# RWKV layers: the outer products of mixes and decays as float32r matmuls over stacked halves, and a product kept in PSUM

## The chip, the cores and the metric

One NeuronCore of a Trainium2 chip runs the whole program. The metric is device time in microseconds (us) of one execution; smaller is better. A matmul runs on TensorE (PE), which loads its weights with a separate instruction (PEld) that can run beside a matmul. VectorE is DVE, ScalarE is ACT, GpSimd is POOL, and SyncE (SP) issues the transfers (DMAs). Each engine works through its own list in order and waits on semaphores for the others.

## What is computed

Input `x` has 16 sequences of 100 steps and 512 channels; `ctx_2048` has 16 sequences of 361. Four layers follow one another: a cross attention with a layer norm (layer 0), an RWKV block (layer 1), a second cross attention with an FFN (layer 2), another RWKV block (layer 3). The change is in the two RWKV blocks only. Cut to what matters, such a block is:

```python
xa = ln(x);  sx = shift(xa) - xa
xxx = tanh((xa + sx * maa_x) @ maa_w1).reshape(b, l, 5, 32)
xxx = einsum('blfd,fde->blfe', xxx, maa_w2)          # five "outer products", 32 deep
xk, xw, xv, xr, xg = xa + sx * (maa_stack + xxx)
w = exp(-exp(time_decay + tanh(xw @ td_w1) @ td_w2)) # one more, 64 deep
r, k, v = xr @ Wr.T, xk @ Wk.T, xv @ Wv.T;  g = silu(xg @ Wg.T)
# per head of 16 channels, over the 100 steps: a = k v^T; out = r (u a + s); s = a + w s
x1 = x + groupnorm(out) * g @ Wo.T
rr = sigmoid(xr2 @ Wfr.T);  kk = relu(xk2 @ Wfk.T) ** 2   # channel mix on ln(x1)
return x1 + rr * (kk @ Wfv.T)
```

## The kernel before

`rwkv(n, ...)` does one RWKV block; it is called for layers 1 and 3. Sequences go in groups of four (`G = 4`, `NG = 4`), so a group has T = 400 columns, and channels go in four chunks of 128 (`NC = 4`). Activations in the projections stand with channels on the 128 partitions and the 400 steps as columns.

**Units.** The recurrence of one chunk of one group is split into eight units of two value rows each: 4 x 4 x 8 = 128 units to a layer. Unit u does: `spread` (two float32r matmuls of 128 x 128 weights `sel` on 400 columns into PSUM tile `vb`, one unit ahead), `product` (DVE copies the first state into `vb`, L1254, and multiplies `vb` by k in place, L1258), `scan` (two DVE scans into tile `a`, L1267; POOL multiplies `a` by r, L1268), and every second unit `gather` (PE sums `a` over channels into `acc`, L1272). `vb` has two tiles, so `spread(u+1)` waits for the scans of unit u-1. The halves of `v` for `spread` were made in the same manner that the change uses: `plain` (L973) rounds v to float32r (`hi`), DVE makes the rest (`lo`), both go to DRAM, and `enter` (L1206) brings them back stacked on 128 rows.

**Pieces.** All other work on PE is cut into pieces, each with a planned cost in us, a first unit (slot) at which it may be taken, and a function that writes its instructions. The loop over u (L1342) runs from -42; before unit 0 only pieces are written. At each u it writes the unit's instructions, then takes pieces from the head of the list until a budget is used: `due = min(due, 0.0) + (2.9 if 0 <= u < UNITS else 3.9)`, less 0.45 in odd units and 0.7 in units 2 and 7 of a chunk (L1390). Cost 0.0 pieces are taken as soon as their slot comes. All engines' programs follow this order.

`projections(g)` (L872) writes the pieces of one group: layer norm and transposes (`turned`, 0.45 each), `inner` (the `maa_w1` product and its tanh into tile `z0`, L936, 2.7), `mixed` (L943: outer products of a pair of mixes, or of one, then DVE's `tm` and POOL's `xj`), `decay_in` (L995: the `td_w1` product together with the last columns of `maa_w1`; tanh into `tz`, L1020), the projections k, v, r (2.7 each), `decay` (L1026) and, held back for the next group's list, the gates g (`held`, then `behind`, 8 half chains of 1.35). Pieces of `behind` stand before `inner` (four) and between the mixes (0,1).

In `mixed` the weights of mix f lie in rows 32f to 32f+32 of `w2a` (f = 4: rows 96 to 128 of `w2b`) and are multiplied with the same rows of `z0` (`tz`), all in float32. `decay` uses rows 0 to 64 of `w2b` and `tz`. A float32 matmul appears in the trace as two records, a float32r matmul as one.

`channels(g)` (L1087) writes the channel mix of a group: layer norm, `keys`, and row products with `gates_of` and `values` (L1155: DVE multiplies the tanh with the product in PSUM into an SBUF tile, then halves and adds x). It starts (L1361) once all four groups are projected. What is left of the pieces after unit 127 runs in the tail. PSUM has three banks for all pieces (`slots`); a bank is read by DVE or ACT before it is used again. `stage` is a ring of six tiles of 128 x 512 for everything on its way to or from DRAM.

## Time and profile before

| what | us |
|---|---|
| three runs: median (lowest to highest) | 3258.19 (3251.58 to 3261.73) |
| the profiled execution | 3254.77 |
| its span, first to last instruction | 3253.0 |
| PE busy / DVE / ACT / POOL in the span | 2949.2 / 1688.9 / 1192.1 / 1157.3 |
| layer 1 about 664 to 1440, layer 3 about 2488 to 3253 | 776, 765 |
| layer 3: first unit starts, last unit starts | 2607.5, 3171.2 |
| layer 1: first unit starts, last unit starts | 784.2, 1351.9 |

How to read the views: a line of the **windows** view gives a stretch, its length, and for PE, PEld, DVE, ACT and POOL the busy time with the number of instructions, then the share of TensorE's clock that was granted, the DMA share and GB/s. A line of the **timeline** gives start, duration, engine, line, operation, output <- inputs with shapes, and a count where neighbours were merged. A line of the **groups** gives line, engine, operation, shapes, count, then busy time, mean ns of one, and the idle time before it with who ended it. The record of a matmul includes its way through the array, so neighbours overlap and the distance between two starts, not the duration, tells what a matmul costs in a dense stretch. L88 and L93 are lines of helpers, so instructions are told apart by their tiles.

### The profile page before, as it was taken

What the parts mean: (1) busy time and instruction counts of PE and PEld (TensorE: products, weight loads), DVE (VectorE), ACT (ScalarE), POOL (GpSimd) and SP (SyncE); (2) the same over time, 40 slices, a digit from 0 to 9 for tenths busy, and PEclk for the clock granted to TensorE, in tenths of its full rate; (3) what the DMA queues carried; (4) which work ended last, traced back from release to release, by engine and by line L of the source; (5) the groups of instructions that cost most, each with busy time, mean ns of one, the idle gap of its engine ahead of it and who ended that gap; (6) DMA issues with size and microseconds to landing.
All of it is one profiled execution on the core that took longest, in us unless ns stands there. A gap on an engine that the chain in (4) does not pass through costs nothing. (4 is left out here: it accounts for less than half of the span.)

```text
span 3253.0 us, 44092 instructions
## 1 busy us (share of the span) xinstructions
PE 2949.2 (91%) x16403; PEld 1497.6 (46%) x16403; DVE 1688.9 (52%) x3565; ACT 1192.1 (37%) x2627; POOL 1157.3 (36%) x966
## 2 busy tenths in 40 slices
PE   7999899888999988879999999899998899998887
PEld 4555555533444434334555555445554444444443
DVE  2555556634888877533433333321001288887871
ACT  4777677721333333322232223211111223333332
POOL 0111111134768666522212111220001267766662
PEclk9999999987999989879999999999998899998988
DMA  6101010021332522120000010020011322332211
GB/s 196 33 23 33 23 36 23 1 90 51 108 102 78 165 76 82 55 88 20 20 21 20 21 30 23 27 71 7 11 50 31 109 91 71 111 128 84 73 53 52
DMA packets 134690, 193.97 MB, mean 60 GB/s; under 512 B 19807, under 2 KB 102687, under 8 KB 134475
## 3 DMA queue, kind: packets, MB, share of 16 engines
q1 hardware_dynamic: 134474, 191.15, 19.1%
q8 instruction: 129, 2.11, 0.3%
q14 instruction: 87, 0.70, 0.1%
HBM read 115.20 MB, written 49.15 MB: 51 GB/s over the span
## 5 line engine op out<-in xcount | busy, mean ns | idle before, releaser
L88 POOL TENSOR_TENSOR a<-a,rc 128x800 f32<-128x800 f32 x256 | 482.0, 1884 | 290.4 <-DVE a L88 174.1
L88 DVE TENSOR_TENSOR_SCAN a<-wc,vb 128x400 f32<-128x400 f32 x512 | 477.3, 974 | 29.0 <-PE acc L93 2.9
L88 DVE CUSTOM_DVE_ANT_0 pr<-l_sc,mask 100x361 f32<-100x361 f32 x512 | 252.2, 529 | 144.7 <-PE l_sc L93 144.6
L88 ACT ACTIVATE pr<-pr,nm 100x361 f32<-100x361 f32 x512 | 301.2, 593 | 4.6 <-POOL sums L88 3.7
L88 DVE TENSOR_TENSOR vb<-vb,kc 128x792 f32<-128x792 f32 x256 | 253.8, 992 | 8.8
L96 PEld LDWEIGHTS l_pT<-ident,pr 100*121 100x121 f32 x1536 | 193.2, 186 | 103.8 <-issue 50.3
L93 PE MATMUL vb<-xc,sel 128*128 128x400 f32 x512 | 221.0, 515 | 14.8 <-DVE a L88 14.7
L1534 DVE CUSTOM_DVE_ANT_0 junk<-l2a_sc,mask 100x361 f32<-100x361 f32 x256 | 136.9, 535 | 182.6 <-PE l2a_sc L93 164.7
L96 PE MATMUL l_pT<-ident,pr 100*121 100x100 f32 x1536 | 216.3, 276 | 6.2 <-ACT pt L88 4.3
L88 POOL TENSOR_TENSOR xj<-tm,ext 128x400 f32<-128x400 f32 x160 | 151.2, 962 | 106.5 <-DVE tm L88 95.5
L1570 POOL TENSOR_TENSOR pa<-pt,pt 121x1600 f32<-121x1600 f32 x16 | 57.1, 3570 | 363.7 <-ACT pt L1565 363.7
L1755 DVE TENSOR_TENSOR x<-pb,x 100x512 f32<-100x512 f32 x16 | 12.9, 805 | 319.6 <-DMA pb<-po 310.8
L88 ACT COPY pt<-l_pT 121x400 f32<-121x400 f32 x256 | 125.1, 489 | 146.5 <-PE l_pT L96 145.5
L93 PE MATMUL v<-l_v_w,ct 128*121 128x512 f32 x384 | 176.9, 605 | 0.0
L74 PE MATMUL h<-yTb,l_fc 128*128 128x400 f32 x512 | 172.8, 499 | 0.6 <-ACT yTb L339 0.6
L93 PE MATMUL k<-ct,l_k_w 128*128 128x361 f32 x512 | 170.6, 476 | 0.0
L88 DVE SCALAR_TENSOR_TENSOR tm<-mm,vec,sx 128x400 f32<-128x400 f32 x160 | 95.4, 623 | 141.3 <-PE mm L93 135.3
L74 PE MATMUL p<-l_proj,h 128*128 128x512 f32 x384 | 165.5, 592 | 0.0
L93 PEld LDWEIGHTS vb<-xc,sel 128*128 128x128 f32 x512 | 99.6, 204 | 125.8 <-issue 61.7
L88 POOL TENSOR_SCALAR ve<-mv 100x1 f32<-100x1 f32 x16 | 3.6, 223 | 406.8 <-DVE mv L88 406.8
L93 PE MATMUL l_sc<-kz,qz 32*100 32x361 f32 x1024 | 112.2, 508 | 34.3 <-DVE nm L88 32.1
L88 DVE COPY pt<-l_pT 121x400 f32<-121x400 f32 x128 | 73.5, 574 | 130.3 <-PE l_pT L96 68.3
(280 smaller groups left out, 5136.0 us busy)
## 6 DMA issues: line engine op xcount, KB each, us to landing
ct<-in_ctxT SPq DMA_DIRECT2D x32, 722.0 KB
dk<-k SPq DMA_DIRECT2D x32, 200.0 KB
kc<-dk SPq DMA_DIRECT2D x32, 200.0 KB
dv<-v SPq DMA_DIRECT2D x32, 200.0 KB
dhi<-hi SPq DMA_DIRECT2D x32, 200.0 KB
dlo<-lo SPq DMA_DIRECT2D x32, 200.0 KB
dw<-wd SPq DMA_DIRECT2D x32, 200.0 KB
vc<-dv SPq DMA_DIRECT2D x32, 200.0 KB
```

What stands on the lines that cost most here:

```text
L74: nc.tensor.matmul(out=ps, lhsT=lhs(c), rhs=rhs(c), start=(c == 0), stop=(c == n - 1))
L88: return lambda *args, **kw: tc.keep_in_program_order(op(*args, **kw))
L93: pin(nc.tensor.matmul(**kw))
L96: pin(nc.tensor.transpose(out, in_, ident))
L1534: nc.vector.tensor_tensor_reduce(out=junk, in0=ss[r][:L, :S2], in1=t["mask"], scale=-1.0, scalar=FLT_MAX, op0=ALU.add, op1=ALU.min, accum_ ...
L1570: nc.gpsimd.tensor_tensor(t["pa"], t["pt"][0], pt, ALU.add)
L1755: nc.vector.tensor_tensor(x, pb[:, i, :], x, ALU.add)
```

## The change

1. The outer products of the mixes and of the decay become float32r matmuls over 128 rows. Weights and tanh are each split in a float32r number and an exact rest. The rows of a mix are stacked hi, lo, hi, lo against weights hi, hi, lo, lo (32 rows each), which gives all four products in one pass; the decay (64 rows deep) takes two passes, one with the weights' hi, one with their lo.
2. The stacked weights are made in the layer itself: `outer_weights` loads each block of rows broadcast over the partitions (6 DMAs), ACT rounds, POOL subtracts. The loads of `w2a` and `w2b` go.
3. `halves` makes hi (ACT) and lo (DVE) of the tanh, and 16 or 6 DMAs per tanh copy the rows to their places in tile `zs`.
4. The first states `s0` are loaded and centered by group instead of once.
5. `values` multiplies into PSUM, and the second product reads PSUM.
6. The planner: pair of mixes 1.0 to 0.6, single mix 0.9 to 0.3, decay 0.9 to 0.6; the budget of a unit 2.9 to 2.65; all gates of the group before stand between `inner` and the mixes; the layer norm of the channel mix of groups 0 and 1 gets a slot three units earlier, with its products where they were.

```diff
-            vec, w1, w2a, w2b, td1, gwb = (small[k] for k in ("vec", "w1", "w2a", "w2b", "td1", "gwb"))
+            vec, w1, td1, gwb = (small[k] for k in ("vec", "w1", "td1", "gwb"))
+            w2 = one.tile([128, 5, E], F32R, name="w2")
+            td2 = one.tile([128, 2, E], F32R, name="td2")
...
+            def outer_weights(f):
+
+                raw = stage(f"w2_{n}_{f}")
+                if f < 5:
+                    nc.sync.dma_start(
+                        out=raw, in_=d[f"L{n}_maa_w2"][32 * f : 32 * f + 32, :].partition_broadcast(4)
+                    )
+                    hi, lo, rs = w2[:, f, :], w2[64:, f, :], slice(64, 128)
+                else:
+                    nc.sync.dma_start(out=raw, in_=d[f"L{n}_td_w2"].partition_broadcast(2))
+                    hi, lo, rs = td2[:, 0, :], td2[:, 1, :], slice(0, 128)
+                scalar.copy(hi, raw)
+                gpsimd.tensor_tensor(lo, raw[rs], plain32(hi[rs]), ALU.subtract)
...
+                s0 = first_states[g] = two.tile([128, NC, G, 16], F32, tag="s0", bufs=3, name=f"s0_{nm}")
+                nc.sync.dma_start(out=s0, in_=d["s0"][:, :, g * G : (g + 1) * G, :])
...
-                        st["z0"] = two.tile([128, T], F32, tag="z0", bufs=1, name=f"z0_{nm}")
-
-                        st["tz"] = two.tile([128, T], F32, tag="tz", bufs=1, name=f"tz_{nm}")
+                        centered(s0.rearrange("p c b s -> p (c b) s"), 16, f"s{nm}")
...
+                def halves(ps, k):
+
+                    z = two.tile([128, T], F32, tag="tm", bufs=4, name=f"z{k}_{nm}")
+                    st["hi", k], st["lo", k] = (stage(f"z{h}{k}_{nm}")[:, :T] for h in ("h", "l"))
+                    scalar.activation(z, ps[:, :T], AF.Tanh)
+                    scalar.copy(st["hi", k].bitcast(F32R), z)
+
+                    def low():
+                        vector.tensor_tensor(st["lo", k].bitcast(F32R), z, st["hi", k], ALU.subtract)
+                        for fs in ((0, 1), (2, 3)) if k == 0 else ((4, 5),):
+                            t = two.tile([128, 2, T], F32R, tag="zs", name=f"zs_{nm}_{fs[0]}")
+                            for i, f in enumerate(fs):
+                                zs[f] = t[:, i, :]
+                                wide = 64 if f == 5 else 32
+                                r0 = 32 * f if f < 4 else 96 if f == 4 else 0
+                                for q in range(128 // wide):
+                                    nc.sync.dma_start(
+                                        out=plain32(t[wide * q : wide * q + wide, i, :]),
+                                        in_=st[("hi", "lo")[q % 2], k][r0 : r0 + wide],
+                                    )
+
+                    stacked[k] = slots.defer(1, low, True)
...
                 def mixed(fs, c):
 
+                    stacked[fs[0] // 4]()
...
-                        mm(out=ps[:, :T], lhsT=w[rs, cols], rhs=z[rs, :], start=True, stop=True)
+                        mm(out=ps[:, :T], lhsT=w2[:, f, cols], rhs=zs[f], start=True, stop=True)
...
                 def decay(co):
 
+                    stacked[1]()
                     ps = slots.bank()
...
+                    for i in range(2):
+                        mm(
+                            out=ps[:, :T], lhsT=td2[:, i, co * 128 : (co + 1) * 128], rhs=zs[5],
+                            start=(i == 0), stop=(i == 1),
+                        )
...
-                pieces.extend(behind[:4])
+                if not g:
+                    for f in range(6):
+                        piece(0.0, lambda f=f: outer_weights(f), base + 2)
                 inner()
+                pieces.extend(behind)
                 for c in range(NC):
                     mix((0, 1), c)
-                    pieces.extend(behind[4 + 2 * c : 6 + 2 * c])
...
-                slot = base + (3 if pace else 1)
+                slot = base + (1, 3, 6)[pace]
...
-                            vector.scalar_tensor_tensor(th, th, 1.0, got, ALU.add, ALU.mult)
-                            vector.scalar_tensor_tensor(x, th, 0.5, x, ALU.mult, ALU.add)
+                            vector.scalar_tensor_tensor(got, th, 1.0, got, ALU.add, ALU.mult)
+                            vector.scalar_tensor_tensor(x, got, 0.5, x, ALU.mult, ALU.add)
...
-                        channel_stream(g, u + (8, 8, 4, 2)[g], g < NG - 1)
+                        channel_stream(g, u + (5, 5, 4, 2)[g], (2, 2, 1, 0)[g])
...
-                due = min(due, 0.0) + (2.9 if 0 <= u < UNITS else 3.9)
+                due = min(due, 0.0) + (2.65 if 0 <= u < UNITS else 3.9)
```

## The prediction

> **What bounds the kernel now.** I read the page first, then the stretches of one RWKV layer in the windows view (layer 3; layer 1 repeats it to within 3%), then PE's timeline, then the waits. In the windows the columns are PE, PEld, DVE, ACT, POOL busy, the clock granted, the DMA share:
>
> ```profile
> 2490.00:2520.00 30.00, 19.71 (x57) 9.49 (x57) 13.51 (x15) 8.30 (x13) 15.80 (x17) 0.60 0.03 10
> 2520.00:2600.00 80.00, 68.92 (x192) 32.59 (x190) 15.55 (x30) 24.65 (x44) 21.32 (x26) 0.88 0.35 111
> 2607.00:3171.00 564.00, 510.88 (x2124) 235.28 (x2126) 465.61 (x674) 191.62 (x315) 389.27 (x304) 0.93 0.28 88
> 3185.00:3253.00 68.00, 53.82 (x282) 26.84 (x282) 12.14 (x24) 16.70 (x29) 13.08 (x18) 0.92 0.14 43
> ```
>
> The first two rows are what comes before unit 0, the third the 127 steps from unit 0's start to unit 127's, the last the tail. Inside the units PE leads with 511 of 564 us, but DVE has 466. One unit costs 564/127 = 4.44 us; counted from the starts of DVE's copies into `vb`, the shortest are 3.0 to 3.1 us, which is DVE's own chain (0.16 + 0.99 + 1.86). So DVE is idle for 98 us of the 564. Who ends that idle time bounds what a faster PE can give:
>
> ```profile
> DVE vb L88 <- PE vb L93: 38.8, 21, 9.2
> PEld mm L93 <- POOL xk_3b L88: 24.2, 10, 5.7
> DVE tm L88 <- PE mm L93: 7.3, 8, 1.8
> ```
>
> Only 38.8 + 7.3 = 46 us of DVE's idle time end with a PE product. Part of these 46 is not PE's speed: where the channel mix waits for POOL's `xk`, PE stands still and `vb` comes late (the longest wait, 9.2 us, ends at 2986.8, right behind such a stop). I put that part at 20 us.
>
> **What an outer product costs.** The timeline of PE, where one merged row holds several records:
>
> ```profile
> 2522.84 0.94 PE L93 MATMUL mm<-z,maa_w2a 32*128 32x400 f32 x4
> 2523.71 2.95 PE L93 MATMUL mm<-xj,l_Wk 128*128 128x400 f32 x8
> 2526.59 0.94 PE L93 MATMUL mm<-z,maa_w2a 32*128 32x400 f32 x4
> ...
> 2527.47 2.95 PE L93 MATMUL mm<-xj,l_Wk 128*128 128x400 f32 x8
> ...
> 2613.55 1.61 PE L93 MATMUL mm<-xj,l_Wk 128*128 128x400 f32 x4
> 2614.69 0.84 PE L93 MATMUL vb<-xc,sel 128*128 128x400 f32 x2
> 2615.36 1.51 PE L93 MATMUL mm<-xj,l_Wk 128*128 128x400 f32 x4
> ```
>
> Four float32 records last 1.51 us with a last one of 0.50, so they start (1.51-0.50)/3 = 0.336 us apart; a float32 product of 400 columns, two records, costs 0.67. The next `l_Wk` after 2523.71 starts at 2527.47: 3.76 us for eight records (2.69) and one pair of mixes, so **a pair costs 1.06**. The decay (2538.73 to 2542.48) and a single mix (2553.72 to 2557.47) show the same 3.75, so 1.06 each: the two of a pair run beside each other, on different rows. The new form is in the trace already: `vb<-xc,sel` is float32r, 128 x 128 weights, 400 columns. The last `l_Wk` before it starts 0.50 us before 2613.55 + 1.61, at 2614.66, and holds the array until 2615.00; the next starts at 2615.36. Two products cost 0.36, **0.18 each**. The other end is where such a pair stands between small weights: 2617.67 to 2618.23, 0.56 or 0.28 each. The neighbours will mostly be 128 x 128, so I take 0.18.
>
> Per layer there are 32 pairs, 16 single mixes and 16 decays. Saved: 32 x (1.06-0.36) + 16 x (1.06-0.18) + 16 x (1.06-0.36) = 22.4 + 14.1 + 11.2 = **48 us of PE** (36 with 0.28 each), 95 us in both layers. The Trainium skill speaks against giving up the small rows ("TensorE: Matmul & The Clock Gate", Part 3: Packing small matmuls): products on different 32-row groups run at the same time, and it advises this for small depth. The trace agrees that they do (a pair costs what a single costs). But the trace's two records to a float32 product still make the pair dearer than two one-pass products; by the page's gap for a warm matmul, 400 columns would take about 0.17 us, an estimate that would make the saving 49 instead of 48.
>
> **Where the 48 us lie.** I went through the planner's list with its printed costs, before and after. Group 0 and group 1's first pairs run before unit 0: 12 pairs, 4 singles, 4 decays. Inside the units remain 20 pairs, 12 singles, 12 decays: 14.0 + 10.6 + 8.4 = 33 us. The smaller budget (2.65) leaves 14.1 planned us after unit 127 instead of 5.5, and half of `decay_in` of group 1 moves ahead of unit 0 (1.4): in all 33 + 8.6 + 1.4 = 43 us less PE work in 128 units, 0.34 a unit.
>
> *In the units.* Not 43, since DVE's 466 us stay: `low` adds 6 x 0.57 (the row of `lo`), the states' centering by group about 3; reading the product from PSUM saves 0.62 for each of about 8 (rows: 1.29 with both operands in SBUF, 0.67 with one in PSUM):
>
> ```profile
> L88 DVE SCALAR_TENSOR_TENSOR cx_1b<-th_1b,cx_1b 128x512 f32<-128x512 f32 x12 | 15.5, 1290 | 0.4
> L88 DVE SCALAR_TENSOR_TENSOR th_1b<-th_1b,mm 128x512 f32<-128x512 f32 x12 | 8.1, 674 | 42.7 <-PE mm L93 42.7
> L88 DVE TENSOR_TENSOR lo<-mm,hi 128x400 fp32r<-128x400 f32 x16 | 9.1, 566 | 19.1 <-ACT hi L88 19.1
> ```
>
> That nets to about zero. So the units can shorten by what DVE waits for PE's work, 46-20 = **26 us**; all 46 if the stops behind `xk` went too; 10 if the bursts eat it (three or four pairs now fit in one unit: 8 x 0.62 on DVE, 8 x 0.96 on POOL, while PE waits for one of three banks). I do not count on the `xk` stops going: the new slot lies three units earlier, but in the planner's list the transposes of groups 0 and 1 still come at units 82-83 and 98, directly before `keys`, since the gates ahead of them are not done sooner.
>
> *Before unit 0.* The tanh's way to PE becomes: tanh 0.50 and rounding 0.50 on ACT, 0.57 on DVE, eight issues on SP before the first pair's tile is whole, then the landing. The rows for the last two:
>
> ```profile
> 2523.46 0.36 SPq L880 DMA_DIRECT2D dk<-k  x1
> 2525.45 0.33 SPq L1219 DMA_DIRECT2D kc<-dk  x1
> ```
>
> The second waits for the first to land: 2.0 us from issue, 0.35 an issue. Sum 0.50 + 0.50 + 0.57 + 8 x 0.35 + 2.0 + about 0.5 of handovers = 6.9, against 0.55 before (tanh starts at 2508.82, PE at 2509.37): **6.3 us more** wherever nothing stands between. In the planner's list that is groups 0 and 1, both before unit 0; groups 2 and 3 have 10.8 planned us of gates between `inner` and the mixes, which cover it (without that cover 6.3 each). 2 x 6.3 = 12.6. Against it: 4 pairs, 4 singles, 4 decays of group 0 save 9.1, and the eight first pairs, which ran at half clock (records 0.67 apart), took 6.2 and 9.3 us and are then set by DVE's 8 x 0.62 = 5.0: 5.5 saved. `outer_weights` adds six ACT copies (0.59, the row of `po<-p`) and six POOL subtractions (1.26, the row of `x<-res`) behind six loads of 256 KB, beside `inner`'s 5.5 us on PE; I add 1 us. A longer halt of PE costs clock: the granted clock is 0.60 in 2490 to 2520, where PE halted for 6.5 and 4.4 us and full spacing is back only at 2518.85; I add 2 us. Total -14.6 + 12.6 + 3 = **+1 us** (-8 to +10). The clock page (same title, Part 1) says that an idle window of about 3.4 us brings the half clock; the trace shows it here after gaps of 4.4 us and more; by the page alone each new halt would cost one window at half speed, an estimate of 1.7 us, 3.4 for both instead of 2.
>
> *The tail.* 8.6 planned us more lie behind unit 127. PE idles 3.4 us there before the last transposes (ended by ACT's `xn_3b`), which cover a part: **+4 us** (0 to 9).
>
> *No cost:* the 22 issues a group, 8 us of SP, stand beside units whose loads are issued four units (18 us) ahead; if a chunk's load came late, its unit would wait as long. The removed loads of `w2a` and `w2b` were hidden in the layers before.
>
> Sum per layer: -26 + 1 + 4 = -21, twice -42: 3254.8 - 42 = 3213 for the profiled execution. The median of the runs lies 3.4 higher, so 3216; I say **3215**.
>
> **Rivals.**
> 1. *PE alone sets the units*: all 43 us come off, and DVE's idle time shrinks to 55. 2 x (-43+1+4) = -76: 3182. For it: PE 511 of 564. Against it: only 46 us of DVE's waits end with PE.
> 2. *DVE takes over*: the bursts of `tm` and POOL's `xj` cost what PE saves; units -10, before unit 0 +5, tail +5: no change, 3258. For it: DVE's 83%, three banks.
> 3. *The stacked tile is late in every group*, slower: SP serves its list in order, so 16 issues waiting for DVE's `low` (written behind a unit's scans, up to 3.1 us) hold the loads of chunks too, and PE halts in the units and goes to half clock. Price per group and layer: 6.3 + 3.1 and about 4 for the clock, 13; over eight groups 107, of which groups 0 and 1 (25) are in the sum: +82-42 = +40, 3298. It decides when the way from tanh to landing passes the gates' cover, about 11 us.
> 4. *It doesn't do what it says*: a float32r product with operands placed by DMA costs like a float32 pass, 0.336. Then per layer 48 pairs and decays save 1.06-0.67 = 0.39 and 16 singles 0.72, 30 in all instead of 48; the units shorten by 26 x 30/48 = 16, and 2 more are lost before unit 0: 2 x (-16+3+4) = -18, 3237.
>
> **How the numbers follow.** Chances: forecast 0.48, rival 1 0.20, rival 2 0.12, rival 3 0.12, rival 4 0.08. The forecast's own ends are 2 x (-46-8+0) = -108 and 2 x (-10+10+9) = +18; I cut at 3165 below, which leaves out little of rival 1, and at 3258 above, which takes in rival 2 and leaves out rival 3. About 0.3% (10 us) is what a measurement of this kernel can tell from no change: faster 0.48 x 0.92 + 0.20 + 0.08 (3237 lies 0.6% below) = 0.72; slower 0.12 and 0.01 of the forecast's upper end = 0.13; within 0.15.
>
> **What would show it.** The records of `mm<-zs,w2` should leave PE 0.18 apart; DVE's busy time should stay within 1%; the 127 unit steps should take about 538 us a layer; the wait of PE for the stacked tile should appear twice a layer, before unit 0, of some 6 us; the page's row of `cx` should fall from 1290 to about 670 ns. Wrong if the units stay at 564 with PE less busy (rival 2), or if PE waits for the stacked tile inside the units (rival 3).

## The result and the profile after

The changed kernel takes 3273.7 us (median of 6 runs, 3270.1 to 3277.2); in the same session the kernel before took 3258.1 (6 runs). The ratio is 1.0052, 95% interval 1.0036 to 1.0068: **slower**, where 3215 and at most 3258 were forecast. The profiled execution took 3275.0 us, its span is 3273.2.

The page of the changed kernel, engines' busy time:

```profile
PE 2869.9 (88%) x16243; PEld 1499.8 (46%) x16243; DVE 1689.0 (52%) x3599; ACT 1207.2 (37%) x2655; POOL 1170.6 (36%) x978
```

PE is busy for 79 us less (95 us of its time were forecast) and DVE for as long as before, as forecast, and yet the span is 20 us longer. So I cut both traces at the same marks (first `xn_a` of a layer, first and last copy into `vb`, last product of layer 1 and end of the span; us, layer 1 / layer 3):

| stretch | before | after | change | forecast a layer |
|---|---|---|---|---|
| start of the layer to unit 0 | 114.4 / 114.0 | 124.7 / 125.8 | +10.3 / +11.8 | +1 |
| 127 unit steps | 567.7 / 563.7 | 560.2 / 553.0 | -7.5 / -10.7 | -26 |
| tail | 80.9 / 81.8 | 85.8 / 87.8 | +4.9 / +6.0 | +4 |

That is +7.7 and +7.1 a layer, 14.8 together, nearly the 15.6 between the medians. Layer 0 is 6.5 us longer in this one profile, with PE's program unchanged there; over all profiles of this study it ends between 669 and 684 us (at 671.0 and 670.4 in a2_slots and f1_both, which hold the change too), so I take it for scatter.

The first two of these stretches of layer 3 in the windows view after (PE, PEld, DVE, ACT, POOL busy; granted clock, DMA share, GB/s):

```profile
2506.60:2632.40 125.80, 81.27 (x236) 44.25 (x238) 32.96 (x56) 37.79 (x66) 48.09 (x54) 0.73 0.34 103
2632.40:3185.40 553.00, 474.79 (x2043) 231.87 (x2042) 461.71 (x681) 193.75 (x319) 389.26 (x304) 0.92 0.31 95
```

In the first row no engine is busy for more than two thirds of the stretch: something is waited for. In the second PE lost 36 us of busy time and the stretch only 11.

**Before unit 0.** ACT's timeline, then PE's, in layer 3 (what stands in brackets is the idle time ahead and who ended it):

```profile
2517.41 0.62 ACT L88 CAST w<-w 128x512 fp32r<-128x512 f32 x1 [1.97 <-DMA w<-in_L_maa_w]
2520.03 0.62 ACT L88 CAST w<-w 128x512 fp32r<-128x512 f32 x1 [2.01 <-DMA w<-in_L_maa_w]
...
2533.11 0.62 ACT L88 CAST td<-w 128x512 fp32r<-128x512 f32 x1 [4.55 <-DMA w<-in_L_td_w]
2533.64 0.50 ACT L88 ACTIVATE z<-mm 128x400 f32<-128x400 f32 x1
```

```profile
2515.75 4.52 PE L93 MATMUL mm<-xm,maa_w 128*128 128x400 f32 x8 [3.78 <-POOL xm L88]
2538.89 0.67 PE L93 MATMUL mm<-zs,w 128*128 128x400 f32 x1 [18.62 <-DMA zs<-zl]
```

The tanh's product ends at 2520.3, but the tanh starts at 2533.64: ACT works in order, and six rounding copies stand ahead of it, each waiting for its load. Five loads land 2.6 us apart, the sixth 5.2 us later. The way from tanh to PE is then 5.3 us, but PE has stood still for 18.6 (18.1 in layer 1). Why loads of 256 KB take that long shows in the view of the DMA engines, 2508 to 2534 in 40 slices (tenths of the 16 engines that are busy, then GB/s):

```profile
DMA  7694110122222222222222222222211111111000
GB/s 163 152 240 95 28 28 1 35 35 19 82 101 98 98 101 104 101 101 101 98 101 101 101 95 101 101 101 98 98 72 50 50 47 50 50 50 50 32 0 0
```

Two tenths at 101 GB/s, then one tenth at 50. The DMA share is 0.26 in 2516 to 2526 and 0.13 in 2528.5 to 2532: about 4 of 16 engines run while a table is broadcast to four blocks of rows, about 2 while one is broadcast to two. The Trainium skill says this ("DMA: Bandwidth & Descriptors", Rules for kernel authors): a transfer whose slowest dimension has c < 16 entries, a leading broadcast of c copies for one, runs on at most c engines. The prediction did not weigh it.

**In the units** the longest new stop is unit 67 (10.8 us; 64 and 66 take 6.6 and 6.8). SP's queue and DVE there:

```profile
2926.81 0.38 SPq L60 DMA_DIRECT2D l_Wfr<-in_L_Wfr  x1
2927.33 0.41 SPq L888 DMA_DIRECT2D dv<-v  x1
```

```profile
2922.86 0.57 DVE L88 TENSOR_TENSOR lo<-mm,hi 128x400 fp32r<-128x400 f32 x1 [2.91 <-DMA dv<-v]
...
2933.65 0.58 DVE L88 TENSOR_TENSOR lo<-mm,hi 128x400 fp32r<-128x400 f32 x1 [7.14 <-issue]
```

DVE waits for the store of the very `v` whose rest it is to write. Four of the six `stage` tiles hold the normalized rows of the channel mix (`xn_3b`, written between 2909.9 and 2920.4), which the new slot brings three units earlier; two are left for `v`, `hi` and `lo`, so `lo` needs a store to have landed. In unit 67 that store lies behind a 1 MB weight load in the queue. That the tile is what is waited for follows from the code and the times; the profile does not name the second wait's releaser here. In layer 3 of b2_onepass_plan (below), which has the new slots and no stacking, DVE stands at the same place for 7.1 us, and there the profile names the store of `v`; in a2_slots, with the old slots, this wait is gone.

**The products themselves** cost what was forecast, with one exception. PE in the dense stretch:

```profile
2557.24 2.95 PE L93 MATMUL mm<-xj,l_Wk 128*128 128x400 f32 x8 [0.22 <-ACT k L88]
2559.72 0.84 PE L93 MATMUL mm<-zs,w 128*128 128x400 f32 x2
2560.78 2.95 PE L93 MATMUL mm<-xj,l_Wk 128*128 128x400 f32 x8 [0.21 <-ACT k L88]
...
2576.67 2.85 PE L93 MATMUL mm<-xj,l_Wr 128*128 128x400 f32 x8
2579.05 0.65 PE L93 MATMUL mm<-zs,w 128*128 128x400 f32 x1
2579.54 2.85 PE L93 MATMUL mm<-xj,l_Wr 128*128 128x400 f32 x8
```

Eight records of a projection are 2.69 us. With a single mix the period is 2.87, so it costs 0.18; a decay (2567.53 to 2570.58) costs 0.36. Both are the prediction's numbers. A pair's period is 3.54, so it costs 0.85 and not 0.36: a pair takes two of the three banks, and the next projection then waits until ACT has copied `k` out of the third. Most of this price is that wait: in e4_thrice (below) four more products in each pair lengthen the period by 0.23 only, to 3.77.

The mean of the product kept in PSUM fell as forecast (1290 ns before):

```profile
L88 DVE SCALAR_TENSOR_TENSOR cx_1b<-mm,cx_1b 128x512 f32<-128x512 f32 x12 | 8.3, 692 | 2.3 <-DMA cx_1b<-x 1.9
```

But the 1290 is a mean of two kinds, so the prediction's "1.29 with both operands in SBUF" is no price of one product. Two of layer 3 before:

```profile
3022.53 3.59 DVE L88 SCALAR_TENSOR_TENSOR cx_3b<-th_3b,cx_3b 128x512 f32<-128x512 f32 x1
...
3201.27 0.69 DVE L88 SCALAR_TENSOR_TENSOR cx_3b<-th_3b,cx_3b 128x512 f32<-128x512 f32 x1
```

Seven of a layer's twelve took 0.69 before as well. The other five took 1.5 to 3.6, all in the units, and these five are the ones that overlap POOL's product of `a`. With one operand in PSUM all twelve take 0.69, beside `a` too.

### The profile page after: what moved, and what is told of

Same layout as the page of the kernel before. It is cut to its first block, busy times and chain, and to the rows that moved or that the text cites. A ratio compares the mean times of both kernels' runs of the same rounds, so it can differ in the third digit from the quotient of the medians.

```text
span 3273.2 us, 44204 instructions
## 1 busy us (share of the span) xinstructions
PE 2869.9 (88%) x16243; PEld 1499.8 (46%) x16243; DVE 1689.0 (52%) x3599; ACT 1207.2 (37%) x2655; POOL 1170.6 (36%) x978
## 5 line engine op out<-in xcount | busy, mean ns | idle before, releaser
L96 PEld LDWEIGHTS l_pT<-ident,pr 100*121 100x121 f32 x1536 | 195.9, 188 | 105.3 <-issue 51.9
L88 ACT COPY pt<-l_pT 121x400 f32<-121x400 f32 x256 | 125.1, 489 | 151.3 <-PE l_pT L96 150.3
L93 PE MATMUL mm<-zs,w 128*128 128x400 f32 x160 | 76.8, 540 | 88.5 <-DMA zs<-zl 52.7
```

The lines of the kernel that those rows point to most:

```text
L88: return lambda *args, **kw: tc.keep_in_program_order(op(*args, **kw))
L93: pin(nc.tensor.matmul(**kw))
L96: pin(nc.tensor.transpose(out, in_, ident))
```

## The experiments

Theories after reading the two traces: **A**, the weights' loads stand in front of the tanh; **B**, three banks; **C**, in the units PE's saving turns into waits (bursts of pairs, `stage` tiles, DVE's in-order waits); **D**, the smaller budget moves work to the tail. The rival to C was the prediction's own step: PE's time counts in the units. All times are medians; each ratio is against the kernel before, run on the same chip. Its median there was 3256.4 for a and b, 3253.6 and 3253.7 for c and d, 3254.4 for e and 3255.2 for f1_both, so a difference of medians between letters is uncertain by some 3 us.

| run | us | ratio (95%) | start to unit 0 | unit steps | 
|---|---|---|---|---|
| a1_late | 3289.7 | 1.0101 (1.0081-1.0121) | 137.1 / 138.9 | 557.8 / 553.4 |
| a2_slots | 3251.3 | 0.9987 (0.9972-1.0003) | 125.1 / 124.6 | 549.8 / 544.6 |
| b1_onepass | 3231.6 | 0.9921 (0.9897-0.9945) | 109.0 / 105.1 | 553.1 / 559.3 |
| b2_onepass_plan | 3239.9 | 0.9940 (0.9919-0.9961) | 109.1 / 105.3 | 556.7 / 556.4 |
| c1_early | 3246.1 | 0.9972 (0.9961-0.9984) | 121.4 / 121.4 | 550.4 / 544.0 |
| c2_budget | 3283.5 | 1.0081 (1.0054-1.0109) | 124.8 / 125.2 | 563.8 / 555.7 |
| c3_pairs | 3281.1 | 1.0079 (1.0056-1.0102) | 124.6 / 124.8 | 560.8 / 559.8 |
| c4_psum | 3245.0 | 0.9968 (0.9953-0.9982) | 114.4 / 114.2 | 563.8 / 557.8 |
| d1_fast | 3241.8 | 0.9957 (0.9943-0.9970) | 118.0 / 117.3 | 550.5 / 544.7 |
| d2_defer | 3246.8 | 0.9973 (0.9955-0.9991) | 124.2 / 124.2 | 549.0 / 541.9 |
| d3_actq | 3235.2 | 0.9941 (0.9921-0.9962) | 114.9 / 115.0 | 551.9 / 545.9 |
| e1_best | 3229.4 | 0.9923 (0.9909-0.9937) | 114.9 / 115.0 | 548.3 / 540.1 |
| e2_pairs | 3246.8 | 0.9977 (0.9965-0.9988) | 125.0 / 124.6 | 541.0 / 543.6 |
| e3_gates | 3267.6 | 1.0041 (1.0027-1.0055) | 123.8 / 125.6 | 557.3 / 551.5 |
| e4_thrice | 3282.5 | 1.0084 (1.0070-1.0097) | 134.3 / 134.0 | 556.9 / 549.5 |
| f1_both | 3228.5 | 0.9915 (0.9901-0.9930) | 113.7 / 114.2 | 544.0 / 547.1 |

### a1_late: the weights in three steps

```diff
-                        piece(0.0, lambda f=f: outer_weights(f), base + 2)
+                        piece(0.0, lambda f=f: outer_weights(f), base + 2 + f // 2)
```

> The changed kernel, with the six outer_weights in three steps of the planner's loop instead of one (f 0 and 1 where they were, 2 and 3 one step later, 4 and 5 two steps later); nothing is left out. Theory A (ACT works in order, so the tanh stands behind six rounding copies whose loads land 2.6 us apart, the last 5.2 us after its neighbour): the tanh stands behind two copies only, PE's longest wait for zs falls from 18.6 to about 7 us, the stretch from the layer's start to unit 0 loses about 10 us in each layer, units and tail stay: 3273 - 20 = 3253. Rival (the loads themselves and the copies of the halves are what is slow, and the wait only moves behind the later loads): the stretch loses under 4 us a layer, 3266 or more.

Theory A fell in this form: 16 us slower than the changed kernel. PE's timeline:

```profile
2529.88 0.42 PE L93 MATMUL mm<-zs,w 128*128 128x400 f32 x1 [5.10 <-DMA zs<-zl]
...
2548.54 0.93 PE L93 MATMUL mm<-xj,td_w 128*64 128x400 f32 x1 [9.53 <-POOL xj L88]
...
2568.56 5.70 PE L93 MATMUL mm<-xj,l_Wk 128*128 128x400 f32 x8 [12.52 <-ACT k L88]
```

The wait for `zs` fell to 5.1, as said. But loads 2 and 3 now stand on SP behind 16 copies of halves (2525.91 to 2536.08, 0.63 us each) and land at 2542 and 2544.6; POOL, in order, stands at their subtraction while `xj` of the first pairs waits (9.5), and ACT does the same at the next two (12.5). The load is the cost wherever it stands.

### a2_slots: the channel mix at its old slots

```diff
-                slot = base + (1, 3, 6)[pace]
+                slot = base + (3 if pace else 1)
-                        channel_stream(g, u + (5, 5, 4, 2)[g], (2, 2, 1, 0)[g])
+                        channel_stream(g, u + (8, 8, 4, 2)[g], g < NG - 1)
```

> The changed kernel with the slots of the channel mix put back as they were before (layer norm and products at the old units); nothing is left out. Theory C (the layer norm of the channel mix, three units earlier, holds four of the six stage tiles while the last group's v, hi and lo need them, and DVE's lo then waits behind a 1 MB weight load: units 64, 66 and 67 take 6.6, 6.8 and 10.8 us): these three come back to about 5 us each, the 127 unit steps lose 5 to 8 us a layer, and the time is 3273 - 13 = 3260. Rival (the stops only change places, since the stop behind xk comes back with the old slot): the unit steps stay within 3 us, 3270 to 3277.

Confirmed and larger: the unit steps lose 10.4 and 8.4 us, the kernel 22 us of its median, and units 64, 66 and 67 take 4.4, 3.5 and 6.6 us. So one edit that was not the products' at all costs 18.8 us in the units of both layers, more than the 15.6 us by which the kernel is slower. PE's waits for `xk` stay (14.1 us in layer 3, 14.2 with the new slots): the earlier slot bought nothing for what it took. A ring with more tiles was not tried, since SBUF has no room for it.

### b1_onepass and b2_onepass_plan: PE's saving without the stacking

In both, `w2a`, `w2b`, `z0` and `tz` become float32r, each rounded once; b2 has the planner of the changed kernel as well.

```diff
-                        st["z0"] = two.tile([128, T], F32, tag="z0", bufs=1, name=f"z0_{nm}")
+                        st["z0"] = two.tile([128, T], F32R, tag="z0", bufs=1, name=f"z0_{nm}")
...
+            for w, raw, rs in ((w2a, raws[0], slice(0, 128)), (w2b, raws[1], slice(0, 64)), (w2b, raws[1], slice(96, 128))):
+                gpsimd.tensor_copy(w[rs], raw[rs])
```

> The kernel before with its outer products alone in one-pass float32r, on 32 (64) rows as before: weights and tanh are rounded once, the exact rests are left out (so the mixes are less accurate), nothing is stacked and no DMA is added behind the tanh; the planner keeps all its old costs, order and budget. PE then loses about what the change saves (48 us a layer, 33 of them in the units) with nothing given back. The prediction's step for the units (DVE's idle time that ends with PE, 26 of 43 us) gives 20 us a layer in the units and 10 to 14 before unit 0: 3258 - 2 x 32 = 3194. Theory B and C (three PSUM banks, DVE's tm and POOL's xj set the pace of a pair, so PE's saving mostly turns into idle time of PE): 9 us a layer in the units and 4 before them: 3232.

> The kernel before with one-pass float32r outer products as in b1_onepass (exact rests left out, mixes less accurate) and with the whole planner of the changed kernel: costs, budget 2.65, gates ahead of the mixes, earlier slots of the channel mix. Against b1_onepass it prices the planner's edits; against the changed kernel it prices the stacking with its DMAs and the weights made in the layer. If the planner's edits cost what theories C and D say (bursts of four pairs, stage tiles, 8.6 us more tail), it is 10 to 25 us slower than b1_onepass; if the planner is an improvement, it is faster than b1_onepass. If the way of z and the outer weights cost only what stands before unit 0 (10 to 16 us a layer), it is 3273 - 2 x 13 = 3247 or so; if the way of z also costs in the units, it is under 3235.

b1 took 3231.6, where C said 3232 and the prediction's step 3194. The saving that the prediction put at 14.6 us before unit 0 measures 5.4 and 8.9, and the units shorten by 14.5 in layer 1 and 4.4 in layer 3. The units of layer 3 in b1 (the prediction shows this stretch of the kernel before, with PE busy for 510.88 us):

```profile
2594.60:3153.90 559.30, 493.03 (x2060) 231.33 (x2060) 465.05 (x675) 190.67 (x315) 390.29 (x305) 0.92 0.29 89
```

PE is busy there for 17.6 us less (24.3 in layer 1), not for the 33 that the expectation names: without the stacking, a single mix on 32 rows or a decay on 64 still costs 0.57 (period 3.26, 2546.28 to 2549.54) and a pair 0.85. By these prices 16 us go in the units, an estimate. So b1 prices cheaper products, but not those of the change.

DVE's waits for PE's `vb` stay in layer 3 (38.8 before). In layer 1 a fifth of them goes. The rows are b1's layer 3, then layer 1 before and in b1:

```profile
DVE vb L88 <- PE vb L93: 38.0, 20, 9.3
```

```profile
DVE vb L88 <- PE vb L93: 39.1, 22, 9.4
```

```profile
DVE vb L88 <- PE vb L93: 30.7, 18, 9.1
```

With the waits of `tm` (7.3 before in either layer; 1.8 and 2.6 in b1), 13.9 of 46 us are gone in layer 1 and 5.5 in layer 3. Within about 1 us that is what the units lost.

b2 against b1: the planner's edits as a whole gain nothing with these products (8 us slower, with overlapping intervals; layer 3's tail is 5.3 longer). b2 against a2_slots, which starts its units 16 and 19 us later, prices stacking and weights before unit 0. Against the changed kernel, which has the same slots, b2's units are 3.5 shorter in layer 1 and 3.4 longer in layer 3, so these runs show no price of the stacking in the units.

### c1_early, d1_fast, d3_actq: the loads, then the queue

c1 issues four of the six broadcast loads at the layer's start into an idle ring and spreads the copies; d1 loads the same bytes with ten transfers of 32 or 64 rows each:

```diff
-                    nc.sync.dma_start(
-                        out=raw, in_=d[f"L{n}_maa_w2"][32 * f : 32 * f + 32, :].partition_broadcast(4)
-                    )
...
+            rows5 = d[f"L{n}_maa_w2"].rearrange("(f p) e -> p f e", p=32)
+            for fs in (slice(0, 3), slice(3, 5)):
+                for q in range(4):
+                    nc.sync.dma_start(
+                        out=raws[fs.start // 3][32 * q : 32 * q + 32, : fs.stop - fs.start, :], in_=rows5[:, fs, :]
+                    )
```

> a2_slots (the changed kernel with the old slots of the channel mix, 3251) with the six loads of outer_weights taken out of the way: they go into the ring of the units' tile a, which stands idle before unit 0, four of them issued at the layer's start, and their ACT and POOL copies are spread over three steps of the planner's loop. Nothing is left out. Theory A, as mended by a1_late (the loads' 2.6 us each are the cost, wherever they stand in front of what needs them: in front of the tanh on ACT in the changed kernel, behind 16 issues of copied halves on SP in a1_late): with the loads done before the transposes, the layer's start to unit 0 falls from 125 to about 113 us, the longest wait of PE for zs from 18.3 to about 7: 3251 - 24 = 3227. Rival (the 16 issues and the rounding of the halves are the larger part): the stretch falls by under 5 us, 3241 or more.

> a2_slots with the same bytes of outer_weights loaded by other transfers: ten, each with 32 (64) rows of the table as its outer dimension instead of a broadcast of 4 (2), issued at the layer's start into two tiles of the ring xm, which stands idle there; the ACT and POOL copies in two steps of the planner's loop. Nothing is left out. Theory A in its last form (a broadcast load whose outer dimension is 4 uses 4 of 16 DMA engines, 256 KB take 2.6 us, and 18 us of such loads delay whatever stands behind them, casts in the changed kernel, copied halves in c1_early): the loads take under 10 us, PE's waits for zs before unit 0 fall from 27.3 to about 2 x 7, the layer's start to unit 0 falls from 125 to 113: 3251 - 24 = 3227. Rival (the copies of the halves alone set the stretch, as c1_early's 121 could also be read): the stretch stays at 119 or more, 3240.

c1 gained 3.7 and 3.2 us of the stretch: its last two loads still stand right ahead of the copied halves in SP's list (2504.93 and 2505.64, the first copy at 2506.33), and PE waited 13.0 us at once. d1 gained 7.1 and 7.3, between the two expectations (113 and 119 against 118.0 and 117.3). The DMA view of d1, 2493 to 2508 in 40 slices, shows the same bytes (and the first states) through in some 9 us:

```profile
DMA  0002889999999999999999999999200000000000
GB/s 0 0 0 16 71 322 361 202 197 186 257 224 202 202 197 262 197 208 251 219 197 251 206 210 197 221 217 219 41 0 0 0 0 0 0 0 0 0 0 0
```

What is left of PE's wait in d1 is the way of the halves:

```profile
2512.17 0.67 PE L93 MATMUL mm<-zs,w 128*128 128x400 f32 x1 [5.18 <-DMA zs<-zl]
2514.75 3.73 PE L93 MATMUL mm<-zs,w 128*128 128x400 f32 x7 [1.91 <-POOL xj L88]
```

5.2 us for the first product, which needs four copies; then 1.9 for the second, which needs four more (the profile names POOL's `xj`, but the two starts lie 2.58 apart, and four issues take 4 x 0.63). A third wait is the weights' again: POOL's second three subtractions stand ahead of `xj`, and PE waits 3.45 us for it at 2524.80. d3 splits the 16 issues over two queues; `copies(queue, h)` issues the copies of the hi (h = 0) or the lo halves:

```diff
+                    ahead = slots.now < 0
+                    if ahead:
+                        copies(nc.scalar, 0)
...
                     def low():
                         vector.tensor_tensor(st["lo", k].bitcast(F32R), z, st["hi", k], ALU.subtract)
-                        for fs in ((0, 1), (2, 3)) if k == 0 else ((4, 5),):
...
+                        if not ahead:
+                            copies(nc.sync, 0)
+                        copies(nc.sync, 1)
```

> d1_fast with the copies of the hi halves issued on ACT's queue right behind the rounding, for the tanhs before unit 0 alone; the lo halves stay on SP. Nothing is left out. If the 0.6 us an issue on one queue set the way of z (the prediction took 0.35), the first pair's tile is whole 2.5 us earlier and the second pair's 5 us earlier, four tanhs a layer: 8 to 12 us less than d1_fast. If landing and waiting for DVE's rest set it, within 3 us of d1_fast.

6.6 us less than d1 in the median, with overlapping intervals, and between the two expectations; the stretch before unit 0 shows 3.1 and 2.3 of it. So the rate of issue is a part of the way. The two waits of PE are 4.3 and 0.8 now. From b1's 107 us (mean) to d3's 115 there remain 8 us a layer. 3.4 of them are PE's wait for `xj` behind POOL's second three subtractions (2512.39 to 2516.23 in layer 3), which is still there; rounding, DVE's rest and the landing were not taken apart further.

### c4_psum: the product in PSUM alone

```diff
-                            vector.scalar_tensor_tensor(th, th, 1.0, got, ALU.add, ALU.mult)
-                            vector.scalar_tensor_tensor(x, th, 0.5, x, ALU.mult, ALU.add)
+                            vector.scalar_tensor_tensor(got, th, 1.0, got, ALU.add, ALU.mult)
+                            vector.scalar_tensor_tensor(x, got, 0.5, x, ALU.mult, ALU.add)
```

> The kernel before with one part of the change alone: the gated values multiplied in PSUM. Nothing is left out. The prediction's term: 0.62 us less of DVE for each of 12 large products a layer (row of cx 1290 to 670 ns), 8 of them in the units, netted against added work as no change of the time: 3257 within 5. Rival (DVE's own chain sets those units, so each 0.62 counts): 2 x 5 to 7 us less, 3245.

The rival held: the units lose 3.9 and 5.8 us and the kernel 8.6. DVE's busy time in the units falls by 8.2 and 7.9 us, more than 8 x 0.62, since the slow products were all there. So half to three quarters of DVE's time counted here.

### e4_thrice: PE's time alone

```diff
-                        mm(out=ps[:, :T], lhsT=w2[:, f, cols], rhs=zs[f], start=True, stop=True)
+                        for _ in range(3):
+                            mm(out=ps[:, :T], lhsT=w2[:, f, cols], rhs=zs[f], start=True, stop=True)
...
-                    for i in range(2):
+                    for i in (0, 1, 0, 1, 0, 1):
```

> a2_slots with every outer product issued three times instead of once (the same result, written again). Nothing is left out. PE then pays 1.1 us for a pair and a decay and 0.5 for a single, about what the kernel before pays; in the units that is 27 us a layer more of PE, and nothing else changes. The prediction's step (26 of 43 us of PE's time in the units count): the units grow by 17 us a layer, 3251 + 2 x 20 = 3291. What b1_onepass showed (33 us less of PE, units shorter by 4 and 15): they grow by 8, 3251 + 2 x 10 = 3271. PE's time hidden behind the other chains altogether: under 3259.

The units of layer 3, a2_slots and e4_thrice:

```profile
2617.60:3162.20 544.60, 475.14 (x2045) 231.83 (x2042) 461.57 (x681) 194.33 (x319) 389.28 (x304) 0.92 0.32 96
```

```profile
2646.30:3195.90 549.60, 491.10 (x2195) 259.97 (x2192) 462.82 (x682) 194.85 (x319) 388.67 (x303) 0.94 0.32 95
```

150 more products are 27 us at 0.18 each. PE's busy time grows by 16.0 us (20.9 in layer 1), as a pair's extra products run while PE would wait for the third bank. The units grow by 5.0 us (7.1 in layer 1): **a third of PE's added busy time counts there**, against 26 of 43 in the prediction. Before unit 0 PE is busy for 10.4 and 12.5 us more and the stretch is 9.2 and 9.4 us longer: there most of PE's time counts. The median rose by 31.2, between the two expectations: about 9 us a layer from the first stretch and 6 from the units.

### d2_defer, e3_gates: the way of the halves in the units

```diff
-                    stacked[k] = slots.defer(1, low, True)
+                    stacked[k] = slots.defer(2, low, True)
```

> a2_slots with low (DVE's subtraction for the tanh's rest, and the copies of the halves) written two units after the tanh instead of one. Nothing is left out. Theory E (DVE works in order and stands at zl for ACT's rounding, 8.7 us in the units of layer 3, up to 4.1 at a time, while its scans wait behind it): these waits vanish, units 20 and 51 lose 4 and 2 us, and the unit steps 4 to 6 us a layer: 3241. Rival (the tile then lands too late for the mixes, and PE waits for zs in the units instead): 3251 or more.

DVE's waits for `zh` in the units of layer 3 (8.7 us in a2_slots) are gone; the units lose 0.8 and 2.7, the kernel 4.5, less than expected and at the edge of what can be told. e3 puts the gates back where they were:

```diff
+                pieces.extend(behind[:4])
                 inner()
-                pieces.extend(behind)
                 for c in range(NC):
                     mix((0, 1), c)
+                    pieces.extend(behind[4 + 2 * c : 6 + 2 * c])
```

> a2_slots with the gates of the group before where the kernel before had them: four half chains ahead of the tanh's product, two behind each first pair. Nothing is left out. The prediction says that the gates between the tanh and the mixes cover the way of z in groups 2 and 3 and that each group without that cover costs 6.3 us: PE then waits for zs in the units, 2 x 6 us a layer, against some 3 us for pairs that no longer come four at a time: 3251 + 2 x 9 = 3269. Rival (DVE's scans of the units run on in the meantime, so the wait is hidden): 3251 within 4.

As the prediction said: without the gates between tanh and mixes, PE waits for the tile in groups 2 and 3.

```profile
PE mm L93 <- DMA zs<-zl: 13.2, 4, 4.9
```

13.2 us for two groups, 6.6 each (6.3 in the prediction), and 13.3 in layer 1. The units are 7.5 and 7.0 us longer, so about half of these waits lengthens them, and the time is 16 us longer. With the gates there the units of a2_slots show no such wait.

### c2_budget, c3_pairs, e2_pairs: bursts, and what is left for the tail

c2 sets the budget to 2.75; c3 to 2.9 and e2 to 2.8, both with costs of 1.2 and 0.6 for a pair and a single mix.

```diff
-                    piece(0.6 if len(fs) > 1 else 0.3, lambda: mixed(fs, c), late)
+                    piece(1.2 if len(fs) > 1 else 0.6, lambda: mixed(fs, c), late)
-                due = min(due, 0.0) + (2.65 if 0 <= u < UNITS else 3.9)
+                due = min(due, 0.0) + (2.8 if 0 <= u < UNITS else 3.9)
```

> a2_slots with a budget of 2.75 in the units instead of 2.65: 3.7 planned us instead of 14.1 are left behind unit 127. Nothing is left out. Theory D (what is left runs in the tail with nothing beside it): the tail of 86.5 to 87.5 us loses 5, the units stretch by 2 or 3: 3251 - 6 = 3245. Rival (the units are bound by PE, so pieces brought into them cost there what they save in the tail): 3251 within 3.

> a2_slots with planned costs of 1.2 for a pair of mixes and 0.6 for a single one (what DVE's tm and POOL's xj of a pair take, instead of PE's time) and a budget of 2.9: 3.7 planned us are left, as in c2_budget. Nothing is left out. Theory C (bursts of four pairs in a unit cost what PE saves): units 20 and 24 of 8.4 and 8.7 us fall to about 5, PE's waits for DVE's tm (9.3 us in the units of layer 3) go below 4, and the 127 steps are 4 to 6 us a layer shorter than in c2_budget: 3235. Rival (the bursts only gather waits that would come anyway): within 4 us of c2_budget.

> a2_slots with planned costs of 1.2 for a pair of mixes and 0.6 for a single one, and a budget of 2.8, so that 15.8 planned us are left behind unit 127, as in a2_slots (14.1); c3_pairs had changed what is left as well. Nothing is left out. If bursts of pairs are what eats PE's saving: units 4 to 6 us a layer shorter, 3241. If they only gather waits that come anyway: 3251 within 4. If the place of the other chains decides more than the pairs do, the time moves by over 5 us in either direction while the number of long units (over 6 us) moves with it.

D fell, and its rival (3251 within 3) too: with ten planned us moved from the tail into the units, the units of c2 grow by 14.0 and 11.1 and the tail loses only 1.6, because the last group's layer norm is late anyway and PE then stands with nothing to do:

```profile
3214.08 0.43 PE L96 MATMUL mm<-ident,xn_3b 100*128 100x100 f32 x1 [10.80 <-ACT xn_3b L88]
```

The work left behind was this wait's cover. c2's profile is of its fastest execution, 18.6 us under its median, so these stretches do not account for all of the 32 us by which the median is longer. c3 has the same shift in it (units +11.0 and +15.2). Against c2 it is level (2.5 us less), as its rival said, but with the shift in both it tells little about bursts. e2 holds what is left: units over 6 us lose a third of their excess over 4 us (62 to 41 a layer, mean), but the others grow from 3.80 to 3.95. Its units are 8.8 and 1.0 us shorter, and the time is 4.5 us under a2_slots with overlapping intervals, between its first two expectations. So these runs show no clear loss by bursts and do not exclude one of a few us. Why c2's units grew by more than the work moved into them (PE is busy there for 9.7 and 5.9 us more) was not traced to one cause: other units are long in it (45, 47 and 117 with 11.3, 12.0 and 13.9 us), with waits for `ox`, `xm`, `zh` and `xk`.

### e1_best and f1_both: what adds up

e1 is d3 with the later `low` of d2 inside the units; f1 adds the costs and the budget of e2.

> d3_actq (old slots of the channel mix, weights loaded by ten transfers, hi halves issued on ACT before unit 0) and the later low of d2_defer inside the units. Nothing is left out. If the gains add (d2_defer took 0.8 and 2.7 us off the units): 3235 - 4 = 3231, against 3254 for the kernel before.

> e1_best with the planned costs and the budget of e2_pairs (pair 1.2, single 0.6, budget 2.8). Nothing is left out. If spreading the pairs takes its gain (units 8.8 and 1.0 us shorter in e2_pairs) from the same waits that the later low already took, the time stays within 4 us of e1_best (3229); if they are separate waits, 3229 - 4 to 8 = 3223; if the order of the other chains decides, it may lose as much.

e1 takes 3229.4 us, 0.9923 (0.9909 to 0.9937) of the kernel before, with the same exact products as the changed kernel: **a version that beats both**. f1's 3228.5 is the same time. That fits its first expectation, that spread pairs and the later `low` take the same waits; but its units are 4.3 us shorter in layer 1 and 7.0 longer in layer 3, so the third, that the order of the other chains decides, is not excluded.

## Why the prediction was wrong

- **Cost of the products** (0.18, 0.36): right for single mixes and decays. A pair costs 0.85 beside a projection, as the trace reads because of the third bank; the prediction named the three banks only for the bursts. At 20 pairs that takes some 10 of the 33 us that PE was to save in the units, an estimate.
- **"In the units ... 26 us"**: the step that failed most. DVE's 46 us of waits that end with PE, less 20 for `xk`, were taken as what a faster PE gives. With b1_onepass's cheaper products 13.9 and 5.5 us of these 46 went, and the units lost 14.5 and 4.4. So what DVE waits for PE is what the units lose, as the prediction said, but the waits of the kernel before do not tell how much of it goes. As the long units read, what stays are stops behind other chains (`xk`, `ox`, `lo`), in which PE waits too; no run isolates them. In e4_thrice a third of PE's added busy time counts. By that third, 12 of the 35 and 37 us by which PE is busy for less in a2_slots's units would count, an estimate.
- **"The new slot lies three units earlier"**, costed at nothing: it cost 10.4 and 8.4 us a layer (a2_slots). As the traces read, that is because the normalized rows take four of six `stage` tiles. The prediction asked what the slot gains and not whose tiles it holds meanwhile. Undone, the kernel would have been level with the one before.
- **"`outer_weights` ... I add 1 us"**: 7.2 us a layer (d1_fast). The six copies were priced, and that the loads are hidden beside `inner` was assumed from their size; they run on 4 and 2 of 16 engines, 18 us in all.
- **The way of z, 6.3 us more**: near the measured size (5.3 us from the tanh to the first product and 7.8 to the second in the changed kernel; 6.6 a group in e3_gates), but partly by luck. Its term of 0.35 an issue measured 0.63, and the first product needs four of the eight issues; the landing is 2.05 from the last issue needed, as forecast. The two queues of d3_actq win 2.7 us a layer.
- **Savings before unit 0, "-14.6"**: 5.4 and 8.9 with b1_onepass's products. Its singles and decays are dearer than the stacked ones; at 0.57 against 0.18 and 0.36 that is 2.4 us, an estimate. As the waits read, the pairs are held there by DVE, POOL and the banks, not by PE alone. With the three points above, +1 became +11: -7 for the products, +7 for the loads, +3 for the queue and +8 for the rest of the way of z and of the weights.
- **Reading PSUM "nets to about zero"**: the saving of 0.62 a product was read from a mean. The slow products were all in the units, where DVE saves 8 us instead of 5, and the units got 4 and 6 of them (c4_psum). What `low` and the states' centering cost against it was not measured alone.
- **Tail +4**: +4.9 and +6.0. The cover of a late layer norm, which the prediction counted, is real (c2_budget).
- **Rivals.** Rival 1 (PE alone sets the units) is refuted by e4_thrice. Rival 2 was nearest in time; its bursts were not shown to cost anything, but its conclusion, that other engines' chains hold most of the units' time, was right. Rival 3's mechanism appears only without the gates (e3_gates). Rival 4 is refuted by the 0.18; its 3237 leaves out the 3.4 us that the other sums add.

The units of a2_slots, the changed kernel with the old slots, are 17.9 and 19.1 us shorter than before. 12 for PE (the estimate above) and 4 to 6 for PSUM make 16 to 18, and the new slots give 10.4 and 8.4 back, which leaves the 7.5 and 10.7 measured. This sum fits but is not proven. Part of what PE is busy for less is work that the planner moved out of the units; c2_budget shows that the budget alone can move them by 11 to 14; and e4_thrice prices time added to the new kernel, not time taken from the old. The planner's edits other than the slots were not separated.

## What to carry to other kernels

- A wait that ends with an engine need not be that engine's slowness: find out what it was waiting for itself before crediting a speedup. Issuing the suspect work three times prices its engine's time; here one of two stretches paid for most of it and the other for a third.
- Look at the outermost dimension of every new transfer, and at what stands behind it in each in-order list (ACT, POOL, SP): here moving a slow load moved its price, and making it wide took 7.2 us a layer off.
- A group's mean can hide two kinds of instruction: before pricing one from it, look at the single ones and at what runs beside the slow ones.
- An edit of the planner that starts something earlier holds its buffers longer; count the ring.

## What the runs showed of the hardware

- 256 KB broadcast to four blocks of rows took 2.6 us at 101 GB/s, to two blocks 5.2 us at 50; the same tables in rows of 32 and 64 ran at some 200 GB/s and more.
- An issue on SP took 0.59 us (0.63 from one to the next) for copies of 32 rows between two SBUF tiles, and 0.32 to 0.44 for the stores of 128 rows. The trace does not say why.
- A DVE product of 128 x 512 with both operands in SBUF took 0.69 us, or 1.5 to 3.6 where it met POOL's product of `a` (ten of ten in the two layers); with one operand in PSUM it took 0.69 beside `a` as well (c4_psum).
- Between projections on 128 rows, a one-pass float32r product cost 0.18 us on 128 rows and 0.57 on 32 or 64 (b1_onepass).
- The granted clock falls to one half inside dense stretches as well. Layer 0, the same PE program, kernel before and changed kernel:

```profile
628.00:636.00 8.00, 6.53 (x52) 4.29 (x48) 5.38 (x19) 6.72 (x22) 0.00 (x0) 1.00 0.00 0
```

```profile
628.00:636.00 8.00, 7.63 (x41) 4.35 (x34) 3.13 (x11) 4.90 (x16) 0.00 (x0) 0.50 0.00 0
```

In the changed kernel the clock was 1.00 until 621, with PE busy for 6.5 of the 8 us before 620 (2.6 of the last 4); its longest halt in the 20 us ahead of the fall is 1.1 us. The clock rule that the prediction cites, an idle window ahead, does not explain this spell. Such a spell stands at other places in other profiles (628 to 644 in b1_onepass). It may make some of the scatter of layer 0; that was not shown.
